# Four paddings ahead of the second score region, two moved steps and a new order of the last list in an attention kernel

## The chip, the cores and the metric

One Trainium2 chip, one of its cores. The metric is the device time of one execution in microseconds (us); lower is better. Several runs of a kernel are summarised by their median. A profile shows one further execution: the time that each instruction took on TensorE (PE for matmuls, PEld for weight loads), VectorE (DVE), ScalarE (ACT), GpSimd (POOL) and the queue of SyncE (SP), which here issues nearly all transfers.

## The reference

Attention with many query heads and one shared key and value head, between two layer norms, added to the input. All is float32.

```python
# x (64, 128, 512); Wq (512, 1024): 16 heads of 64; cond (64, 64): rows 0 and 1 are the null key
# and value, and it stands for Wkv (512, 128); attn_bias (16, 128, 128); mask (64, 128); Wo (1024, 512)
xn = layernorm(x, g_in)
q = (xn @ Wq).reshape(b, n, H, DH).transpose(0, 2, 1, 3) * DH ** -0.5
k, v = split(xn @ Wkv)
k, v = concat([null_key, k], 1), concat([null_value, v], 1)
sim = einsum('bhid,bjd->bhij', q, k) + concat([null_bias, attn_bias], -1)
sim = where(causal_mask, neg, sim)
sim = where(mask (the null column is always allowed), sim, neg)
out = einsum('bhij,bjd->bhid', softmax(sim), v)
return x + layernorm(out.reshape(b, n, H * DH) @ Wo, g_out)
```

## The kernel before

There are B = 64 batch entries of 128 tokens. The kernel works on them in pairs, in cycles `c`: while cycle `c` does the softmax of the batches 2c and 2c+1, it also projects the queries of a later group of four batches, does the output projection of the pair before, the final norm of the pair before that, and loads and normalises tokens five pairs ahead. The order of all of it is written out by hand: each engine runs its instructions in the order of the source, and an engine waits where another has not yet delivered.

- `cycle(c)` is one such pass for c = 1 to 29. It ends in `region(c)`: the scores of the batches 2c+2 and 2c+3 (`heads`, line 651) and the values of 2c and 2c+1 (`values_one`, line 770), 128 and 112 PE matmuls on 64- and 32-row tiles of the array, of which several run at a time. `region(-1)` and `region(0)` stand in a front part that is written out apart; region(0) is the second run of scores.
- Projections use Strassen's scheme: `q_one(c, k, h)` is product `k` of seven for the queries, `out_one(p, k)` product `k` of seven for the outputs of the pair `p`. In the cycles from LEAF = 2 on three of the query products are split once more (`leaf(c, k, stage)`, matmuls on line 553, additions by DVE on line 556). In the first two cycles the products 1, 6, 7 and 4 of `q_one` (line 597) are accumulated in one PSUM bank, `pa`, and ACT copies the bank between them (lines 608 and 614).
- One matmul of the source is four PE instructions, two weight loads and two matmuls; one output product has four such matmuls, `q_half` and `kv_mm` too, one query product has two, and the stages 0 to 3 of a leaf have one, three, two and one.
- The softmax of a half `hf` of a batch is `scores_max` (DVE), `exps` (ACT, line 701, eight rows), `rinv` (DVE, a reciprocal, line 718), `scale` (POOL, line 722); then `blocks_T` (DVE, line 737) transposes the batch for the values. `bias_add` (POOL, line 635) prepares the scores' bias.
- Tokens go through DVE's 32x32 transposes, one store of a group to DRAM (`tokens_out`, 1 MB, line 340) and loads back (`tokens_in`). In the front, `tokens_out(2)` is the last statement before `region(0)`.
- `nc.tensor.addr_align(256, offset=n)` pads PE's instructions with fillers (NOP in the profile) until the next one stands at place `n` of a block of 256. Three stand in the front (lines 1397, 1406, 1419), at 30, 71 and 135; one in each cycle (line 1240), at 133, 129, 143 and 152 in the cycles 1 to 4, at 141 in the last and at 159 in the others, ahead of `leaf(c, 4, 1)`.
- After the last cycle a hand-written list finishes the last eight batches. Their output norm is `pair_stats` (DVE: statistics, line 909, their aggregation, 911, and a sum, 913), `pair_pow` (POOL, 917), `pair_center` (DVE, line 942: subtract the mean, multiply by the gain `gob`), `pair_scale` (DVE, line 948: scale, add the residual `res`), `store`. The functions `gain_copy` (ACT copies the gain to a PSUM bank, which `pair_center` then reads) and `stats_part` (the statistics of half a row) exist, but are not called.

Of the kernel before, what the change touches and what calls it, by code (L numbers as in the profile page):

```python
# [17 lines left out]
def kernel(  # L18
# [940 lines left out]
    def store(b):  # L959
        nc.sync.dma_start(out=out[b], in_=ys.pop(b))  # L960
# [12 lines left out]
    def q_one(c, k, h):  # L973
        i = 2 * c + 4 + h
        g, f = divmod(i, GB)
        if g >= NG:
            return
        if k == 1 and f % FH == 0:
            q_tile(g, f // FH)
        if k == 1:  # L980
            product(g, f, 1, ps_q, "a")
            if c >= LEAF:
                first_into(g, f, 0)
            else:
                keep("a", "p1")
        elif k == 2:
            product(g, f, 2, ps_w, "w")
            q_out(g, f, lo_t, "w", "p1")
        elif k == 5:
            product(g, f, 5, ps_q, "c")  # L990
        elif k == 6:
            product(g, f, 6, ps_q, "a", start=False)
            if c >= LEAF:
                first_into(g, f, 1)
            else:
                keep("a", "u2")
        elif k == 7:
            product(g, f, 7, ps_q, "a", start=False)
            if c >= LEAF:
                first_into(g, HC + f, 0)  # L1000
                nc.vector.tensor_tensor(
                    q_part(g, HC + f, 1), by_block("c"), q_part(g, HC + f, 0), ALU.add
                )
            else:
                keep("a", "u3")
                q_out(g, HC + f, hi_t, "c", "u3")
        elif k == 8:
            o = q_part(g, f, 1)
            nc.vector.tensor_tensor(o, by_block("c"), o, ALU.add)
        elif k == 3:  # L1010
            product(g, f, 3, ps_q, "c", start=False)
            q_out(g, f, hi_t, "c", "u2")
        else:
            product(g, f, 4, ps_q, "a", start=False)
            q_out(g, HC + f, lo_t, "a")

    def out_one(p, k, dve=False):
        if not 0 <= p < B:
            return
        if k == 1:  # L1020
            out_product(p, 1, ps_y, "X")
            out_keep("yp1", 1, dve)
        elif k == 2:
            out_product(p, 2, ps_w, "w")
            out_part(p, 0, "w", "yp1")
        elif k == 6:
            out_product(p, 6, ps_y, "X", start=False)
            out_keep("yu2", 2, dve)
        elif k == 5:
            out_product(p, 5, ps_y, "Y")  # L1030
        elif k == 7:
            out_product(p, 7, ps_y, "X", start=False)
            out_keep("yu3", 1, dve)
            out_part(p + 1, 1, "Y", "yu3")
        elif k == 4 and at_end:
            out_product(p, 4, ps_w, "w")
            out_part(p + 1, 0, "w", "yu3")
        elif k == 3 and at_end:
            out_part(p, 1, "Y", "yu2")
            out_product(p, 3, ps_w, "w")  # L1040
            o = y_half(p, 1)
            nc.vector.tensor_tensor(o, prod["yw"], o, ALU.add)  # L1042
# [28 lines left out]
    def cycle(c):  # L1071
# [70 lines left out]
            mask_neg(n0 // GB)  # L1142
        if c >= LEAF:
            q_one(c, 8, 0)
        out_one(p, 2)
        if toks:
            norm_stats(m)
        if soft:
            exps(b0, 1, 0, 6)
        if c < LEAF:  # L1150
            q_one(c, 4, 0)
        q_one(c, 1, 1)
        if c >= LEAF:
            leaf(c, 2, 1)
# [67 lines left out]
            blocks_T(b0)  # L1222
        if fin:
            store(r + 1)
        if soft:
            rinv(b1, 1)
            scale(b1, 1)
        q_one(c, 5, 1)
        if c >= LEAF:
            leaf(c, 4, 0)  # L1230
        q_one(c, 7, 1)
        if c >= LEAF:
            q_one(c, 8, 1)
# [3 lines left out]
            bias_add(n0)  # L1237
        out_one(p, 7)
        if soft:
            nc.tensor.addr_align(256, offset={1: 133, 2: 129, 3: 143, 4: 152, B // 2 - 3: 141}.get(c, 159))  # L1240
        if c >= LEAF:
            leaf(c, 4, 1)
        if soft:
# [172 lines left out]
    tokens_T(9)  # L1416
    leaf_weights(2, 2)
    q_one(0, 6, 1)
    nc.tensor.addr_align(256, offset=135)
# [43 lines left out]
    scores_max(B - 4, 1)  # L1463
    exps(B - 4, 0, 0, 8)
    scores_upper(B - 2, ps_w, "ww")
    exps(B - 4, 1, 0, 8)
    scores_add(B - 2, 1)
    scores_max(B - 3, 1)
    out_one(B - 6, 1, True)
    rinv(B - 4, 0)  # L1470
    out_one(B - 6, 2)
    out_sum(B - 6, 1)
    out_sum(B - 6, 2)
    scores_add(B - 2, 0)
    scale(B - 4, 0)
    rinv(B - 4, 1)
    scores_max(B - 2, 0)
    exps(B - 3, 0, 0, 8)
    scores_upper(B - 1, ps_s, "s")
    scale(B - 4, 1)  # L1480
    out_one(B - 6, 5)
    scores_add(B - 1, 1)
    load_res(B - 6)
    exps(B - 3, 1, 0, 8)
    scores_add(B - 1, 0)
    blocks_T(B - 4)
    out_sum(B - 6, 3)
    out_one(B - 6, 6, True)
    rinv(B - 3, 0)
    scores_max(B - 2, 1)  # L1490
    scale(B - 3, 0)
    load_res(B - 5)
    rinv(B - 3, 1)
    pair_stats(B - 8)
    out_one(B - 6, 3)
    banks = value_banks(B - 4, True)
    scale(B - 3, 1)
    blocks_T(B - 3)
    values_one(B - 4, 0, banks)
    exps(B - 2, 0, 0, 8)  # L1500
    values_out(B - 4, (0, 2))
    values_out(B - 4, (1, 3))
    scores_max(B - 1, 0)
    rinv(B - 2, 0)
    out_one(B - 6, 7, True)
    out_one(B - 6, 4)
    exps(B - 2, 1, 0, 5)
    values_one(B - 3, 1, banks)
    values_out(B - 3, (0, 2))
    scale(B - 2, 0)  # L1510
    pair_pow(B - 8)
    values_out(B - 3, (1, 3), True)
    out_sum(B - 4, 0)
    exps(B - 2, 1, 5, 8)
    pair_stats(B - 7)
    rinv(B - 2, 1)
    exps(B - 1, 0, 0, 8)
    scores_max(B - 1, 1)
    banks = value_banks(B - 2, True)
    out_one(B - 4, 1, True)  # L1520
    scale(B - 2, 1)
    rinv(B - 1, 0)
    blocks_T(B - 2)
    pair_center(B - 8)
    out_one(B - 4, 2)
    pair_scale(B - 8)
    store(B - 8)
    exps(B - 1, 1, 0, 8)
    out_sum(B - 4, 1)
    out_one(B - 4, 5)  # L1530
    out_sum(B - 4, 3)
    rinv(B - 1, 1)
    pair_stats(B - 6)
    pair_stats(B - 5)
    out_one(B - 4, 6)
    out_one(B - 4, 3)
    values_one(B - 2, 0, banks)
    out_sum(B - 4, 2)
    scale(B - 1, 1)
    values_out(B - 2, (0, 2), True)  # L1540
    pair_pow(B - 7)
    scale(B - 1, 0)
    values_out(B - 2, (1, 3))
    pair_pow(B - 5)
    blocks_T(B - 1)
    pair_center(B - 7)
    out_one(B - 4, 7)
# [81 lines left out]
```

## Time and profile before

| | before |
|---|---|
| median of 3 runs | 1040.87 us (1039.3 to 1042.82) |
| the profiled execution | 1039.45 us, its span 1037.7 us |
| PE busy | 1018.7 us, 98% |
| PEld busy | 894.7 us, 86% |
| DVE busy | 862.6 us, 83% |
| POOL busy | 788.3 us, 76% |
| ACT busy | 644.2 us, 62% |
| mean granted clock of PE | 0.996 |

The span runs from the first to the last instruction; the execution's own time has 1.75 us more around it. The busy time of an engine is the time in which at least one of its instructions ran. PEclk is the clock that PE was granted, as a share of full speed. In rows of groups, "x6 | 7.1, 1191 | 0.0" reads: six instructions, 7.1 us busy in all, 1191 ns each in the mean, 0.0 us of idle time before them; in rows of a timeline, start and duration in us, engine, line, operation, output and inputs, and in brackets the idle time before it and what ended that. In the list of waits, "a <- b: 5.3, 14, 0.5" is the total in us, how many, and the longest. In a table of stretches the columns are named in its head, "(x129)" counting instructions.

### The profile page before, as it was taken

To read this page: it belongs to the slowest core of one execution; us is meant where nothing else is said; L and a number is where in the kernel's file an instruction comes from. 1 tells how busy PE (TensorE), PEld (TensorE's weight loads), DVE (VectorE), ACT (ScalarE), POOL (GpSimd) and SP (SyncE) were. 2 spreads that over 40 slices of the span, in tenths; PEclk is the share of its full clock that TensorE was granted. 3 is DMA by queue.
4 is the path that set the end of the run, shared out by engine and by line. 5 is a ranking of instruction groups with operands and counts; after the bars stand their busy time and mean duration, and the time that the engine had idled before them with its cause. 6 is when DMAs were issued, how large, how long until landed. Compare 5 with 4: busy or idle time off the path is not lost. (4 is left out here: it accounts for less than half of the span.)

```text
span 1037.7 us, 31779 instructions
## 1 busy us (share of the span) xinstructions
PE 1018.7 (98%) x12104; PEld 894.7 (86%) x12104; DVE 862.6 (83%) x1996; ACT 644.2 (62%) x2743; POOL 788.3 (76%) x710
## 2 busy tenths in 40 slices
PE   8989999999999999999999999999999999999996
PEld 7878888888888888888888888898888898888875
DVE  7765888888888888888888888888888988878788
ACT  3646765557765657756557765567755567765581
POOL 3697959779595886968779596886968779596774
PEclk9999999999999999999999999999999999999999
DMA  6551151531606225051431615225151441502202
GB/s 211 162 129 48 52 136 53 138 101 73 161 17 160 69 92 146 32 156 53 130 109 72 148 31 148 81 85 153 33 156 53 130 109 73 125 13 63 83 11 92
DMA packets 70263, 100.90 MB, mean 97 GB/s; under 512 B 27744, under 2 KB 31328, under 8 KB 68320
## 3 DMA queue, kind: packets, MB, share of 16 engines
q1 hardware_dynamic: 69008, 97.83, 33.5%
q8 instruction: 96, 1.57, 0.7%
q10 hardware_dynamic: 1104, 1.05, 0.3%
q14 instruction: 55, 0.45, 0.1%
HBM read 63.19 MB, written 33.55 MB: 93 GB/s over the span
## 5 line engine op out<-in xcount | busy, mean ns | idle before, releaser
L701 ACT ACTIVATE s<-s,nmax 128x65 f32<-128x65 f32 (+1 forms) x1024 | 377.0, 401 | 3.2 <-DVE nmax L692 3.2
L701 ACT ACTIVATION_READ_ACCUMULATOR s<-s,nmax 128x1 f32 x1024 | 229.8, 224 | 0.0
L722 POOL TENSOR_TENSOR s<-s,rinv 128x1024 f32<-128x1024 f32 (+1 forms) x128 | 188.3, 1481 | 50.5 <-DVE rinv L718 49.8
L635 POOL TENSOR_TENSOR s<-biasp,mneg 128x1552 f32<-128x1552 f32 x64 | 204.9, 3223 | 2.3 <-DMA x<-in_x_dram 2.0
L810 ACT ACTIVATE oT<-poX,nv 128x256 f32<-128x256 f32 x59 | 28.0, 475 | 224.3 <-PE poX L770 117.8
L556 DVE TENSOR_TENSOR qT<-pl,qT 128x128 f32<-128x128 f32 (+1 forms) x420 | 128.5, 329 | 9.1 <-PE pl L553 6.6
L687 DVE TENSOR_TENSOR s<-ps,s 128x256 f32<-128x256 f32 (+2 forms) x224 | 120.1, 606 | 15.9 <-PE ps L651 15.2
L860 PE MATMUL pyX<-wo,oT 128*128 128x256 f32 x512 | 121.6, 380 | 0.3 <-POOL oT L843 0.3
L692 DVE TENSOR_REDUCE nmax<-s 128x8 f32<-128x520 f32 (+1 forms) x128 | 118.9, 950 | 0.0
L860 PE MATMUL pyX<-wT,oT 128*128 128x256 f32 x488 | 115.5, 380 | 0.3 <-POOL oT L843 0.3
L737 DVE STREAM_TRANSPOSE sb<-s 128x1536 f32<-128x1536 f32 x64 | 112.9, 1765 | 0.5 <-POOL s L722 0.5
L860 PEld LDWEIGHTS pyX<-wo,oT 128*128 128x128 f32 x512 | 96.7, 190 | 15.4 <-issue 1.3
L917 POOL TENSOR_TENSOR rstdo<-rstdo,nhalf 128x1 f32<-128x1 f32 x64 | 36.7, 574 | 81.9 <-PE pl L553 70.0
L860 PEld LDWEIGHTS pyX<-wT,oT 128*128 128x128 f32 x488 | 88.4, 190 | 10.4 <-POOL oT L843 0.7
L651 PE MATMUL ps<-kT,qT 64*64 64x128 f32 (+1 forms) x4096 | 93.6, 245 | 0.7 <-issue 0.7
L651 PEld LDWEIGHTS ps<-kT,qT 64*64 64x64 f32 x4096 | 85.5, 134 | 5.7 <-issue 2.4
L289 POOL TENSOR_TENSOR rstd<-rstd,nhalf 128x1 f32<-128x1 f32 x64 | 37.3, 584 | 67.4 <-DVE rstd L288 65.4
L770 PE MATMUL pos<-sb,vr 32*64 32x128 f32 (+1 forms) x1792 | 83.8, 325 | 2.8 <-issue 2.8
L770 PE MATMUL poY<-sb,vr 32*64 32x128 f32 x720 | 76.7, 352 | 0.0
L770 PE MATMUL poX<-sb,vr 32*64 32x128 f32 x960 | 75.7, 304 | 0.0
L503 ACT COPY qT<-pa 128x256 f32<-128x256 f32 x168 | 66.7, 397 | 1.4 <-PE pa L597 1.4
L860 PE MATMUL pyw<-wo,oT 128*128 128x256 f32 x280 | 66.3, 379 | 0.6 <-POOL oT L843 0.6
(147 smaller groups left out, 2514.5 us busy)
## 6 DMA issues: line engine op xcount, KB each, us to landing
res<-in_x_dram SPq DMA_DIRECT2D x64, 256.0 KB, 3.1
out_dram<-y SPq DMA_DIRECT2D x58, 256.0 KB, 2.0
x<-in_x_dram SPq DMA_DIRECT2D x224, 64.0 KB, 2.7
xd<-xb SPq DMA_DIRECT2D x14, 1024.0 KB, 3.9
xT<-xd SPq DMA_DIRECT2D x56, 256.0 KB, 5.7
vr<-vd SPq DMA_DIRECT2D x64, 128.0 KB, 2.7
x<-in_x_dram SPq DMA_DIRECT2D x8, 256.0 KB, 4.8
vd<-vt SPq DMA_DIRECT2D x32, 64.0 KB, 2.2
```

What stands on the lines that cost most here:

```text
L289: nc.gpsimd.tensor_tensor(rstd, rstd, nhalf, ALU.pow)
L503: nc.scalar.copy(q_part(g, c, h), by_block("a"))
L556: nc.vector.tensor_tensor(o, p, o, ALU.add)
L635: nc.gpsimd.tensor_tensor(S[b], biasp, mneg[:, t].unsqueeze(1).broadcast_to([P, R8, ROW]), ALU.add,)
L651: nc.tensor.matmul(to[r][i * DH : (i + 1) * DH, f, :], qT[g, f // FH, t // GH][rows, f % FH, t % GH, NQ - 1 - i if hf else i], kT[g][rows, ...
L687: nc.vector.tensor_tensor(sv, ps, sv, ALU.add)
L692: nc.vector.tensor_reduce(nmax[b][:, hf], S[b][:, :, WITH_NULL[hf]], AX.X, ALU.max, negate=True)
L701: nc.scalar.activation(row, row, AF.Exp, bias=nmax[b][:, hf, k : k + 1], accum_out=rsum[b][:, hf, k : k + 1],)
L722: nc.gpsimd.tensor_tensor(sv, sv, rinvs.pop((b, hf)).unsqueeze(2).broadcast_to([P, R8, sv.shape[2]]), ALU.mult,)
L737: nc.vector.transpose(sb.rearrange("p j e q -> p e j q"), S[b][:, :, 1 : ROW - 1].rearrange("p e (j k) -> p e j k", k=Q),)
L770: nc.tensor.matmul(po[s][rows, half], vr[g][quad(s), j, t, :], sb[quad(s), slots, r * NF : (r + 1) * NF, :], start=start, stop=True, skip_ ...
L860: nc.tensor.matmul(prod[key], h[:, c, :], w[:, c, :], start=(start and c == 0), stop=(c == HC - 1), skip_group_check=not start,)
```

## The change

- In the front the three paddings go to 31, 73 and 138, and a fourth, to 179, is put ahead of `q_half(2, 1)`.
- In the cycles the paddings 133, 129, 143 and 152 become 159 like the others.
- In `cycle`, `q_one(c, 4, 0)`, which only the second cycle (c = 1) has, moves ahead of `out_one(p, 2)`, `norm_stats` and six exponentials. The reciprocal `rinv(b1, 1)` and its `scale` move behind `q_one(c, 5, 1)` and `leaf(c, 4, 0)`.
- The list behind the last cycle has a new order. It now calls `gain_copy()` once, behind the values of B - 1, and `stats_part` for the last two batches; `values_out(B - 6, (0, 2))` and the evacuation in `out_one(B - 4, 7)` go from ACT to DVE, those in `out_one(B - 4, 1)` from DVE to ACT; `load_res(B - 6)`, which takes one of two buffers that the residuals of B - 8 and B - 7 hold, now stands behind `load_res(B - 5)`, which takes the other; PE's only new order is `out_one(B - 4, 3)` behind `values_one(B - 2, 0)`.

```diff
@@ -1142,13 +1142,13 @@
             mask_neg(n0 // GB)
         if c >= LEAF:
             q_one(c, 8, 0)
+        else:
+            q_one(c, 4, 0)
         out_one(p, 2)
         if toks:
             norm_stats(m)
         if soft:
             exps(b0, 1, 0, 6)
-        if c < LEAF:
-            q_one(c, 4, 0)
         q_one(c, 1, 1)
         if c >= LEAF:
             leaf(c, 2, 1)
@@ -1222,12 +1222,12 @@
             blocks_T(b0)
         if fin:
             store(r + 1)
-        if soft:
-            rinv(b1, 1)
-            scale(b1, 1)
         q_one(c, 5, 1)
         if c >= LEAF:
             leaf(c, 4, 0)
+        if soft:
+            rinv(b1, 1)
+            scale(b1, 1)
         q_one(c, 7, 1)
         if c >= LEAF:
             q_one(c, 8, 1)
@@ -1237,7 +1237,7 @@
             bias_add(n0)
         out_one(p, 7)
         if soft:
-            nc.tensor.addr_align(256, offset={1: 133, 2: 129, 3: 143, 4: 152, B // 2 - 3: 141}.get(c, 159))
+            nc.tensor.addr_align(256, offset={B // 2 - 3: 141}.get(c, 159))
         if c >= LEAF:
             leaf(c, 4, 1)
         if soft:
@@ -1394,7 +1394,7 @@
     rinv(1, 0)
     q_half(0, 1)
     scale(1, 0)
-    nc.tensor.addr_align(256, offset=30)
+    nc.tensor.addr_align(256, offset=31)
     q_one(0, 4, 0)
     exps(1, 1, 0, 4)
     exps(1, 1, 4)
@@ -1403,7 +1403,7 @@
     rinv(1, 1)
     q_one(0, 3, 0)
     scale(1, 1)
-    nc.tensor.addr_align(256, offset=71)
+    nc.tensor.addr_align(256, offset=73)
     q_one(0, 1, 1)
     q_one(0, 2, 1)
     out_weight_sum(0)
@@ -1416,13 +1416,14 @@
     tokens_T(9)
     leaf_weights(2, 2)
     q_one(0, 6, 1)
-    nc.tensor.addr_align(256, offset=135)
+    nc.tensor.addr_align(256, offset=138)
     q_one(0, 5, 1)
     q_one(0, 7, 1)
     out_weight_sum(1)
     values_send(1)
     norm_apply(10)
     norm_apply(11)
+    nc.tensor.addr_align(256, offset=179)
     q_half(2, 1)
     blocks_T(1)
     bias_add(3)
@@ -1447,145 +1448,150 @@
         cycle(c)
     at_end.append({})
 
-    load_res(B - 4)
-    load_res(B - 3)
+    scores_lower((B - 2, B - 1))
+    scores_max(B - 4, 0)
+    values_out(B - 6, (1, 3))
     load_res(B - 2)
-    load_res(B - 1)
-    values_out(B - 6, (1, 3))
-    values_out(B - 6, (0, 2))
-    scores_max(B - 4, 0)
-    scores_max(B - 3, 0)
-    bias_add(B - 1)
-    scores_lower((B - 2, B - 1))
+    values_out(B - 6, (0, 2), True)
     values_out(B - 5, (1, 3), True)
     values_out(B - 5, (0, 2), True)
-    out_sum(B - 6, 0)
     scores_max(B - 4, 1)
...
     values_one(B - 1, 1, banks)
+    pair_stats(B - 4)
+    store(B - 8)
     values_out(B - 1, (0, 2))
-    pair_center(B - 5)
+    pair_pow(B - 7)
+    pair_center(B - 7)
     pair_scale(B - 7)
-    store(B - 7)
     values_out(B - 1, (1, 3))
-    pair_stats(B - 4)
-    pair_stats(B - 3)
+    gain_copy()
     pair_pow(B - 6)
     out_one(B - 2, 1)
-    out_sum(B - 2, 0)
-    out_sum(B - 2, 1)
+    store(B - 7)
+    pair_stats(B - 3)
     pair_center(B - 6)
     out_one(B - 2, 2)
+    out_sum(B - 2, 0)
+    pair_center(B - 5)
+    out_sum(B - 2, 1)
     out_sum(B - 2, 3)
     pair_pow(B - 3)
     pair_center(B - 3)
-    pair_pow(B - 4)
     pair_scale(B - 6)
     store(B - 6)
+    pair_scale(B - 3)
+    store(B - 3)
     pair_scale(B - 5)
     store(B - 5)
+    pair_pow(B - 4)
+    out_sum(B - 2, 2)
     pair_center(B - 4)
-    pair_scale(B - 3)
-    store(B - 3)
     out_one(B - 2, 5)
+    pair_scale(B - 4)
+    store(B - 4)
     out_one(B - 2, 6)
     out_one(B - 2, 3)
-    pair_scale(B - 4)
-    store(B - 4)
-    out_sum(B - 2, 2)
+    stats_part(B - 2, 0)
+    stats_part(B - 2, 1)
     pair_stats(B - 2)
     pair_pow(B - 2)
     pair_center(B - 2)
     pair_scale(B - 2)
-    store(B - 2)
     out_one(B - 2, 7)
     out_one(B - 2, 4)
+    stats_part(B - 1, 1)
+    stats_part(B - 1, 0)
     pair_stats(B - 1)
     pair_pow(B - 1)
+    store(B - 2)
     pair_center(B - 1)
     pair_scale(B - 1)
     store(B - 1)
```

More of the change, by code (lines that the diff above doesn't have):

```diff
@@ L1224, in cycle @@
             store(r + 1)
+        q_one(c, 5, 1)
+        if c >= LEAF:
+            leaf(c, 4, 0)
         if soft:
@@ L1227, in cycle @@
             scale(b1, 1)
-        q_one(c, 5, 1)
-        if c >= LEAF:
-            leaf(c, 4, 0)
         q_one(c, 7, 1)
@@ L1448 @@
     at_end.append({})
-    load_res(B - 4)
-    load_res(B - 3)
+    scores_lower((B - 2, B - 1))
+    scores_max(B - 4, 0)
+    values_out(B - 6, (1, 3))
     load_res(B - 2)
-    load_res(B - 1)
-    values_out(B - 6, (1, 3))
-    values_out(B - 6, (0, 2))
-    scores_max(B - 4, 0)
-    scores_max(B - 3, 0)
-    bias_add(B - 1)
-    scores_lower((B - 2, B - 1))
+    values_out(B - 6, (0, 2), True)
     values_out(B - 5, (1, 3), True)
     values_out(B - 5, (0, 2), True)
-    out_sum(B - 6, 0)
     scores_max(B - 4, 1)
+    scores_upper(B - 2, ps_w, "ww")
+    scores_max(B - 3, 0)
     exps(B - 4, 0, 0, 8)
-    scores_upper(B - 2, ps_w, "ww")
+    load_res(B - 4)
+    load_res(B - 1)
     exps(B - 4, 1, 0, 8)
     scores_add(B - 2, 1)
+    bias_add(B - 1)
+    load_res(B - 3)
     scores_max(B - 3, 1)
     out_one(B - 6, 1, True)
-    rinv(B - 4, 0)
-    out_one(B - 6, 2)
+    out_sum(B - 6, 0)
     out_sum(B - 6, 1)
     out_sum(B - 6, 2)
+    rinv(B - 4, 0)
+    rinv(B - 4, 1)
     scores_add(B - 2, 0)
-    scale(B - 4, 0)
-    rinv(B - 4, 1)
     scores_max(B - 2, 0)
     exps(B - 3, 0, 0, 8)
[L1479 to L1483, printed above, removed]
+    scale(B - 4, 0)
     exps(B - 3, 1, 0, 8)
     scores_add(B - 1, 0)
+    out_one(B - 6, 2)
+    scores_upper(B - 1, ps_s, "s")
+    out_one(B - 6, 5)
+    scale(B - 4, 1)
+    out_sum(B - 6, 3)
+    scores_add(B - 1, 1)
     blocks_T(B - 4)
-    out_sum(B - 6, 3)
     out_one(B - 6, 6, True)
     rinv(B - 3, 0)
+    load_res(B - 5)
+    scale(B - 3, 0)
     scores_max(B - 2, 1)
-    scale(B - 3, 0)
-    load_res(B - 5)
+    exps(B - 2, 0, 0, 8)
     rinv(B - 3, 1)
+    scale(B - 3, 1)
+    load_res(B - 6)
+    out_one(B - 6, 3)
     pair_stats(B - 8)
-    out_one(B - 6, 3)
+    pair_pow(B - 8)
     banks = value_banks(B - 4, True)
-    scale(B - 3, 1)
-    blocks_T(B - 3)
     values_one(B - 4, 0, banks)
-    exps(B - 2, 0, 0, 8)
     values_out(B - 4, (0, 2))
     values_out(B - 4, (1, 3))
-    scores_max(B - 1, 0)
-    rinv(B - 2, 0)
+    blocks_T(B - 3)
     out_one(B - 6, 7, True)
@@ L1507 @@
     exps(B - 2, 1, 0, 5)
+    exps(B - 2, 1, 5, 8)
+    rinv(B - 2, 0)
+    scale(B - 2, 0)
     values_one(B - 3, 1, banks)
+    scores_max(B - 1, 0)
     values_out(B - 3, (0, 2))
-    scale(B - 2, 0)
-    pair_pow(B - 8)
     values_out(B - 3, (1, 3), True)
     out_sum(B - 4, 0)
-    exps(B - 2, 1, 5, 8)
-    pair_stats(B - 7)
     rinv(B - 2, 1)
     exps(B - 1, 0, 0, 8)
+    out_one(B - 4, 1)
+    pair_stats(B - 7)
     scores_max(B - 1, 1)
-    banks = value_banks(B - 2, True)
-    out_one(B - 4, 1, True)
+    exps(B - 1, 1, 0, 8)
+    pair_center(B - 8)
     scale(B - 2, 1)
     rinv(B - 1, 0)
+    out_one(B - 4, 2)
     blocks_T(B - 2)
[L1524 to L1528, printed above, removed]
     out_sum(B - 4, 1)
-    out_one(B - 4, 5)
-    out_sum(B - 4, 3)
+    banks = value_banks(B - 2, True)
     rinv(B - 1, 1)
```

17 lines of the change are left out of this document (9 added, 8 removed).

## The prediction, made before the changed kernel was run

> **What bounds the kernel now.** I read the page's head first, then a table of stretches, then the rows behind the one odd stretch, and the end last.
>
> ```profile
> span 1037.7 us, 31779 instructions
> ...
> PE 1018.7 (98%) x12104; PEld 894.7 (86%) x12104; DVE 862.6 (83%) x1996; ACT 644.2 (62%) x2743; POOL 788.3 (76%) x710
> ...
> q8 instruction: 96, 1.57, 0.7%
> ```
>
> TensorE (PE) is busy 98% of the span, the next engine 83%: what shortens PE's own time shortens the kernel, and what only another engine waits for does not. The third line is the fetch of code: 96 packets, 1.57 MB in all, thus 16 KB each, for 12104 matmuls, as many weight loads and a few hundred instructions of the sequencer, so one packet is a block of about 256. A padding sets the next instruction's place in such a block, its slot; the table compares the same work at different slots. Each pass ends in a region of 128 score matmuls and 112 value matmuls, 64 or 32 rows each, so several run at once and instructions are used up fastest there.
>
> ```profile
> core 0: us, PE busy (x) PEld busy (x) DVE busy (x) ACT busy (x) POOL busy (x), PEclk, DMA share, GB/s
> 63.95:66.79 2.84, 2.84 (x129) 2.67 (x128) 2.09 (x4) 0.00 (x0) 2.84 (x2) 1.00 0.94 355
> 66.79:67.69 0.90, 0.90 (x32) 0.44 (x28) 0.24 (x2) 0.00 (x0) 0.90 (x2) 1.00 0.47 122
> 67.69:70.36 2.67, 0.00 (x0) 0.00 (x1) 2.67 (x6) 0.00 (x0) 2.67 (x2) 0.96 0.51 118
> 70.36:74.01 3.65, 3.65 (x84) 3.10 (x84) 1.60 (x2) 0.00 (x0) 3.57 (x4) 0.56 0.98 230
> 101.04:106.66 5.62, 5.62 (x241) 4.79 (x241) 4.79 (x10) 0.00 (x0) 5.62 (x4) 1.00 0.02 6
> 132.52:138.14 5.62, 5.62 (x241) 4.88 (x240) 5.56 (x13) 0.00 (x0) 1.80 (x1) 1.00 0.36 64
> 163.97:169.54 5.57, 5.57 (x242) 4.88 (x241) 4.81 (x12) 0.00 (x0) 5.57 (x4) 1.00 0.03 7
> 195.34:200.64 5.30, 5.30 (x242) 4.71 (x241) 5.24 (x12) 0.00 (x0) 1.95 (x1) 1.00 0.43 78
> 258.45:263.74 5.29, 5.29 (x241) 4.71 (x240) 5.23 (x12) 0.00 (x0) 1.93 (x1) 1.00 0.45 99
> 195.34:227.35 32.01, 31.79 (x379) 27.39 (x378) 27.24 (x66) 20.19 (x86) 18.78 (x15) 1.00 0.55 135
> 289.49:320.58 31.09, 31.09 (x379) 27.62 (x378) 26.36 (x63) 20.20 (x86) 29.31 (x31) 1.00 0.16 61
> 320.58:352.08 31.50, 31.41 (x379) 27.47 (x378) 27.24 (x66) 20.18 (x86) 18.78 (x15) 1.00 0.56 137
> ```
>
> Rows 1 to 4 are region(0), in pieces: 2.84 + 0.90 + 2.67 + 3.65 = 10.06 us; rows 5 to 9 are regions 1, 2, 3, 4 and 6: 5.62, 5.62, 5.57, 5.30, 5.29. Region(0) thus loses 4.77 us: 2.67 in which PE does nothing, and most of the rest at a granted clock of 0.56.
>
> The code says where the gap lies. One matmul call of the source is two matmuls and two weight loads, four slots. After the padding to 135 come 2 + 2 + 4 + 4 + 2 + 2 = 16 calls, 64 slots: region(0) starts at slot 199. 256 slots of scores, one semaphore instruction and the 28 weight loads of row 2 with their 28 matmuls end at 199 + 256 + 1 + 56 = 512, exactly a block's edge. PE ran out of instructions. The same count puts regions 1 to 4 at slots 181, 197, 211, 220 and all later ones but one at 227.
>
> Why only there? The block behind an edge is fetched when the sequencer passes the edge before (slot 256, in the scores).
>
> ```profile
> 63.53 0.35 SPq L340 DMA_DIRECT2D xd<-xb  x1
> ...
> q1 hardware_dynamic: 217, 1.04, 93.9%
> ...
> q8 instruction: 1, 0.02, 27.5%
> ...
> q8 instruction: 1, 0.02, 24.6%
> ...
> q8 instruction: 1, 0.02, 28.8%
> ...
> 602.14 1.10 PE L651 MATMUL ps<-kT,qT 64*64 64x128 f32 x32
> ```
>
> The first row is SyncE's timeline: a 1 MB store is issued 0.4 us before region(0). The second is the DMA table for 64.4 to 67.5: the engines are 94% busy with it. The third is that table for 67.9 to 68.1: only then does the block's fetch move, and 2.3 us later PE resumes. The fourth (257.9 to 258.2) and fifth (602.7 to 602.9) are the fetches of two regions at slot 227, whose scores began at 258.45 and, by the last row, at 602.14; no gap followed in either. My reading: in region(0) the fetch queued behind the 1 MB.
>
> The Trainium skill, "Runtime: NRT & Kernel Launch", section Instruction fetch mechanics, says that the cost of crossing a 16 KiB boundary is "mostly hidden". By that rule this change would bring next to nothing in the front; 512 being hit exactly speaks against it here.
>
> **The change part by part** (against the profiled execution's 1039.45 us; its span is 1037.7).
>
> *Region(0).* The new padding puts slot 179 before 4 + 4 + 2 + 2 calls: 179 + 48 = 227, as in the steady regions. The edge in the scores is passed 28 instructions sooner. If, as in the row at 258, the fetch moves 0.45 us before the scores, then with scores at about 64.2 it moves near 63.75, ahead of the 1 MB (from 64.4). As late as at 602.8, 0.7 after its scores' start, it would be caught again. I take the former: like region(6) at 258, and unlike region(17), region(0) has scores that need nothing of the last few products before it. 10.06 to 5.29, **-4.77**. That the slow clock goes too rests on the row behind the gap: 0.56 after a gap of 2.67, 1.00 in all other stretches.
>
> The Trainium skill, "TensorE: Matmul & The Clock Gate", section What's actually happening, has the clock halve after about 3.4 us of idleness; the trace shows it after 2.67. If the rule held and the slow clock had another cause, 84 matmuls at 5.29's pace (2.45 us for 112) would keep their 1.8 us of loss, and the whole would come out 1.8 higher.
>
> *The pads' own cost.*
>
> ```profile
> L1419 PEldq NOP  x24: 13/13/13, 55.1 to 56.8; - x24
> ...
> 56.88 1.10 PE L597 MATMUL pc<-xS,wS 128*128 128x256 f32 x4 [0.52 <-DVE xb L331]
> ...
> 58.68 3.62 PE L437 MATMUL pq<-xT,wq 128*128 128x256 f32 x16
> ```
>
> 24 fillers take 1.7 us, 0.07 each, and PE starts right behind the last. By the slots, the three old pads grow by one filler each and the new one holds 179 - 138 - 16 = 25, some 1.85 us. They begin when the eight matmuls before them are queued, and those keep PE busy from 56.88 to 58.68. Cost between 0.2 and 2.0 on the path; I take **+0.3**, as 1.8 us of work stand over 1.85 of fillers. If that cover were gone it would be the 2.0.
>
> *The per-pass pads.* In the second cycle 12 calls, 48 slots, follow its pad, in later ones 17 calls, 68. Region 1 goes from 133 + 48 = 181 to 159 + 48 = 207, between rows of 5.62 and 5.57: nothing. Regions 2 and 3 go to 227: 0.33 + 0.28 = **-0.6**. Region 4 gains 0.01.
>
> *The moved product* (second cycle only, c = 1).
>
> ```profile
> 79.30 1.03 PE L597 MATMUL pa<-xS,wq 128*128 128x256 f32 x4
> 80.16 1.89 PE L860 MATMUL pyw<-wo,oT 128*128 128x256 f32 x8
> ...
> 83.51 0.48 PE L597 MATMUL pa<-xT,wq 128*128 128x256 f32 x1 [0.59 <-ACT qT L614]
> ...
> 80.47 0.43 ACT L608 COPY ku<-pa 128x256 f32<-128x256 f32 x1
> ```
>
> Product 4's evacuation no longer queues behind six exponentials, so the 0.59 wait goes. But product 4 adds into the bank that ACT is copying until 80.90, and the product that covered this (80.16 on) now comes after it: PE would wait from 80.16 to about 81.0, 0.8. **0**, between -0.6 and +0.3. Behind the wait are queued only PE's own products; the six exponentials start later, and their reciprocal has room.
>
> *The moved reciprocal.*
>
> ```profile
> 346.06 0.16 DVE L718 RECIPROCAL rinv<-rsum 128x8 f32<-128x8 f32 x1
> 346.14 0.23 DVE L556 TENSOR_TENSOR qT<-pl,qT 128x128 f32<-128x128 f32 x1
> ...
> 346.42 0.30 PEld L553 LDWEIGHTS pl<-xS,wq 128*128 128x128 f32 x2 [0.49 <-DVE qT L556]
> ...
> PEld pl L553 <- DVE qT L556: 5.3, 14, 0.5
> ```
>
> PE waits for the addition, which stands behind the reciprocal. Swapped, it starts 0.08 us sooner; six or so of the waits are of this kind (31.50 against 31.09 in the table): **-0.4**, between 0 and -0.5. POOL's scaling starts 0.2 later, before two bias additions with nothing near them that PE waits for.
>
> *The final list.* PE's order hardly changes, and its work not at all; DVE's tail decides.
>
> ```profile
> L942 DVE SCALAR_TENSOR_TENSOR y_end<-y_end,mvo,gob 128x512 f32<-128x512 f32 x6 | 7.1, 1191 | 0.0
> L948 DVE SCALAR_TENSOR_TENSOR y_end<-y_end,rstdo,res 128x512 f32<-128x512 f32 x6 | 4.4, 744 | 0.9 <-POOL rstdo L917 0.9
> L948 DVE SCALAR_TENSOR_TENSOR y<-y,rstdo,res 128x512 f32<-128x512 f32 x2 | 2.2, 1085 | 0.0
> ...
> 1027.05 0.42 DVE L1042 TENSOR_TENSOR y_end<-pyw,y_end 128x256 f32<-128x256 f32 x1
> 1027.28 1.89 PE L860 MATMUL pyw<-wT,oT 128*128 128x256 f32 x8
> 1033.89 0.75 DVE L948 SCALAR_TENSOR_TENSOR y_end<-y_end,rstdo,res 128x512 f32<-128x512 f32 x1 [0.44 <-POOL rstdo L917]
> ```
>
> PE is done at 1029.17, the last DVE result at 1034.64: DVE runs through its list in order. The six centerings that now read the gain from PSUM took 1191 ns each, the residual steps of the same shape 744; at 744 they save 6 x 0.45 = 2.7. No row shows a centering with a PSUM gain; if it is no faster, 0. Added to DVE ahead of the last half: one evacuation (0.35, as ACT gives it up) and residual steps that now run beside POOL's sums, which took 1085 instead of 744 (three: 1.0). Halved statistics change nothing: both halves still stand behind the last addition. -2.7 + 0.35 + 1.0 = **-1.4**, between -2.7 and +0.8 (the load of the third residual row block now waits for the second residual step; its landing can hold up DVE).
>
> Sum: -4.77 + 0.3 - 0.6 + 0 - 0.4 - 1.4 = **-6.9**: 1032.6 beside 1039.45. The median of the three runs, 1040.87, lies 1.4 above that execution, so I forecast 1034.0. Nothing should give it back: the steady passes are PE-bound (31.09 busy of 31.09).
>
> **The rivals.**
>
> *The fetch is caught again* (19%). For: the margin is 0.65 us, and the row at 602.8 is late by more. Then the 4.77 stay: -2.1, **1038.8**. Against: the row at 258.
>
> *Crossings cost nothing here* (3%), the rule above: the gap has another cause, and again 1038.8. Against: slot 512.
>
> *The waits for x become the rule* (6%), the slower case.
>
> ```profile
> DVE st L284 <- DMA x<-in_x_dram: 7.5, 12, 1.3
> ```
>
> In passes like 320.58 to 352.08 DVE waits for a token load and is then late for PE, at 0.41 us a pass, and 0.92 in the pass from 195.34. Some 22 passes are free of it. All passes begin earlier against the loads' queue; if every one fell into this, 22 x 0.92 less 6.9 is +13, at half of that +3. It decides from (6.9 + 3.1) / 22 = 0.45 a pass; I give it **1045**. Against: each load is issued in its pass's own order, so it moves along.
>
> **How the numbers follow.** My forecast has 72%: 1034.0, with -9.0 to -3.2 from the ends above, 1031.9 to 1037.7. The range reaches on to the first rival: 1031.5 to 1039.0. A measurement here tells 0.3% (3.1 us) from no change; 1037.7 is that edge. Faster: 0.72 and a little of the first rival, 0.75. Same: the rest of that and the second rival, 0.17. Slower: the third and some unnamed, 0.08.
>
> **What would show it.** Region(0) near 5.3 us with PEclk 1.00 and a code packet before 64.4; regions 2 and 3 at 5.29; fewer of the 0.25 us waits of PE for DVE's L556; a wait of 0.8 us before product 4 in the second cycle; centerings near 0.74 us and the distance from PE's end to the last DVE result shorter than 5.5. A gap of over 2 us in region(0) would prove the main term wrong; centerings still near 1.2 us the tail's.

## The result, and the profile after

The changed kernel takes 1034.44 us (median of 5 runs, 1031.49 to 1035.38), the kernel before 1040.68 us beside it (5 runs, 1039.3 to 1042.82). The ratio is 0.9934, its 95% interval 0.9915 to 0.9954: 6.2 us, or 0.66%, faster. The forecast was 1034.0, a sum of -6.9.

The profiled execution took 1035.38 us, the longest of the five, its span 1033.6. The head of its page, and then the code queue:

```profile
span 1033.6 us, 31778 instructions
...
PE 1017.9 (98%) x12104; PEld 894.1 (87%) x12104; DVE 864.3 (84%) x2000; ACT 644.0 (62%) x2742; POOL 787.5 (76%) x710
...
q8 instruction: 96, 1.57, 0.7%
```

PE is busy 0.8 us less, while the span is 4.1 us shorter: what went was mostly time in which PE stood still. These two profiles differ by less than the medians do; the section on the prediction says why in part. The code packets are as many as before. The table of stretches for regions 0, 1, 2 and 3, then for one odd and one even pass (a pass is a cycle, counted from one region's start to the next; an odd one ends in a region of odd number):

```profile
core 0: us, PE busy (x) PEld busy (x) DVE busy (x) ACT busy (x) POOL busy (x), PEclk, DMA share, GB/s
64.36:69.65 5.29, 5.29 (x241) 4.71 (x240) 4.09 (x8) 0.00 (x0) 5.29 (x3) 1.00 0.78 263
96.70:102.63 5.93, 5.71 (x242) 4.91 (x241) 5.12 (x10) 0.00 (x0) 5.93 (x4) 1.00 0.03 6
128.45:133.74 5.29, 5.29 (x241) 4.71 (x241) 5.23 (x12) 0.00 (x0) 2.12 (x1) 1.00 0.39 68
159.57:165.13 5.56, 5.56 (x242) 4.83 (x241) 4.80 (x12) 0.00 (x0) 5.56 (x4) 1.00 0.03 7
628.44:661.03 32.59, 31.84 (x379) 27.39 (x379) 27.27 (x66) 20.19 (x86) 18.70 (x15) 1.00 0.54 132
661.03:692.13 31.10, 31.10 (x379) 27.63 (x379) 26.39 (x63) 20.20 (x86) 29.82 (x31) 1.00 0.17 62
```

Region(0) takes 5.29 us instead of 10.06, has no gap and runs at full clock. The DMA table for 63.6 to 63.8 holds its code packet (first row below), 0.7 us ahead of its scores; SyncE issues the 1 MB store at 63.81 (second row), behind it.

```profile
q8 instruction: 1, 0.02, 29.5%
...
63.81 0.35 SPq L340 DMA_DIRECT2D xd<-xb  x1
```

Region(2) is at 5.29 as forecast, region(3) at 5.56 is not, and region(1) is slower (5.62 to 5.93). The odd pass of the fifth row is 1.5 us longer than a pass needs. The list of waits of the whole span shows a possible cause, and the moved product's new wait:

```profile
DVE st L284 <- DMA x<-in_x_dram: 9.4, 11, 2.0
...
PEld pl L553 <- DVE qT L556: 6.4, 14, 1.0
...
PE pa L597 <- ACT ku L608: 0.6, 1, 0.6
```

VectorE waits for token loads 9.4 us in all (7.5 before), and PE for VectorE's additions 6.4 us, 14 times (5.3 before, 14 times). The end, as groups, as POOL's last power, and as VectorE's last addition and last result:

```profile
L948 DVE SCALAR_TENSOR_TENSOR y_end<-y_end,rstdo,res 128x512 f32<-128x512 f32 x6 | 5.6, 943 | 0.7 <-POOL rstdo L917 0.4
L942 DVE SCALAR_TENSOR_TENSOR y_end<-y_end,mvo,gain 128x512 f32<-128x512 f32 x6 | 4.3, 737 | 0.0
L948 DVE SCALAR_TENSOR_TENSOR y<-y,rstdo,res 128x512 f32<-128x512 f32 x2 | 2.8, 1382 | 0.1
...
1029.23 0.55 POOL L917 TENSOR_TENSOR rstdo<-rstdo,nhalf 128x1 f32<-128x1 f32 x1 [2.77 <-DVE rstdo L913]
...
1024.32 0.42 DVE L1042 TENSOR_TENSOR y_end<-pyw,y_end 128x256 f32<-128x256 f32 x1
1029.84 0.75 DVE L948 SCALAR_TENSOR_TENSOR y_end<-y_end,rstdo,res 128x512 f32<-128x512 f32 x1
```

From the last addition to the last result it is 6.27 us (1024.32 to 1030.59), before 7.59 (1027.05 to 1034.64).

### The profile page after: what moved, and what is told of

Read it like the earlier page. It is cut to its first block, busy times and chain, and to the rows that moved or that the text cites. A ratio compares the mean times of both kernels' runs of the same rounds, so it can differ in the third digit from the quotient of the medians.

```text
span 1033.6 us, 31778 instructions
## 1 busy us (share of the span) xinstructions
PE 1017.9 (98%) x12104; PEld 894.1 (87%) x12104; DVE 864.3 (84%) x2000; ACT 644.0 (62%) x2742; POOL 787.5 (76%) x710
## 5 line engine op out<-in xcount | busy, mean ns | idle before, releaser
L556 DVE TENSOR_TENSOR qT<-pl,qT 128x128 f32<-128x128 f32 (+1 forms) x420 | 128.6, 329 | 9.5 <-PE pl L553 6.9
```

Of the source, the lines that this page charges most:

```text
L556: nc.vector.tensor_tensor(o, p, o, ALU.add)
```

## The experiments

Four came first: the paddings alone, all but the paddings, the store at another place, and the list alone.

**The paddings alone.**

```diff
 (the kernel before)
-    nc.tensor.addr_align(256, offset=30)
+    nc.tensor.addr_align(256, offset=31)
...  71 to 73, 135 to 138
+    nc.tensor.addr_align(256, offset=179)
     q_half(2, 1)
...
-  offset={1: 133, 2: 129, 3: 143, 4: 152, B // 2 - 3: 141}.get(c, 159)
+  offset={B // 2 - 3: 141}.get(c, 159)
```

> The kernel before with the four front paddings and the paddings of the cycles 1 to 4 of the changed kernel, and nothing else. Theory (the paddings carry the gain, by taking region(0)'s code fetch out from behind the 1 MB store): region(0) 10.06 to about 5.3 us without a gap and without half clock, region(1) up by 0.3 (5.9, as in the changed kernel), regions 2 and 3 together down by 0.3; about -4.8 us in all, less what the waits for x give back: between -4.8 and -3. Rival (block edges cost nothing, the gain comes from the steps and the list): within 1 us of the kernel before, the gap of 2.67 us stays somewhere in the front.

Measured: 1035.24 us against 1040.33, ratio 0.9952 (0.9939 to 0.9965), -5.1 us. Regions 0 and 1:

```profile
64.73:70.02 5.29, 5.29 (x241) 4.71 (x240) 4.09 (x8) 0.00 (x0) 5.29 (x3) 1.00 0.82 263
97.03:103.12 6.09, 5.70 (x241) 4.90 (x240) 5.26 (x10) 0.00 (x0) 6.09 (x4) 1.00 0.02 5
```

The paddings carry most of the gain, and region(1) is slower by them alone. The median lies just past the expected band, on the side of more gain.

**All but the paddings.** The changed kernel with the seven old paddings and without the fourth.

> The changed kernel with the paddings of the kernel before. Theory: region(0) is back near 10 us with its gap of about 2.7 and its half clock, and only the list, the reciprocal and the moved product are left: -1 to -1.8 us against the kernel before. Rival (the list and the steps carry the gain): -4 us or more, region(0) short.

Measured: 1039.45 us against 1040.33, ratio 0.999 (0.9979 to 1.0001); region(0) 9.75 us, at a clock of 0.82 in the mean. The rest of the change is worth about 0.9 us, a little under the expected band, and the interval just reaches zero.

**The store behind region(0) in the source.**

```diff
-    tokens_out(2)
     region(0)
+    tokens_out(2)
```

> The kernel before, with the 1 MB store issued behind region(0) instead of ahead of it; all slots as before, region(0) at 199 and its second edge at exactly 512. Theory A (the fetch of the block behind 512 is asked for at 256, in the scores, and waits behind the 1 MB): with the queues empty region(0) takes 5.3 to 5.9 us, no gap over 0.6 and no half clock; about -4.5 us, if the loads that follow the store are not late. Rival B (the edge at 512 itself, where it falls between the last weight load and the last matmul of a row of scores, or the prefetch depth there): the gap of 2.67 us and 10.06 stay with free queues. Rival C (both): a gap of 1 to 2 us.

Measured: 1041.17 us, ratio 1.0005 (0.9994 to 1.0016), region(0) 9.52 us. SyncE's timeline shows that the experiment changed nothing:

```profile
63.73 0.35 SPq L340 DMA_DIRECT2D xd<-xb  x1
```

Region(0) issues no transfer, so on SyncE's queue the store has the same neighbours as before, and goes out 0.4 us ahead of the scores again. The run tells none of the theories apart.

**The list alone.** The kernel before with the new list behind the last cycle, `gain_copy()` and `stats_part` included, and nothing else.

> The kernel before with the new order of the final list, its gain copied to PSUM and the half statistics, nothing else. Theory: from the start of region(29) to the end about 1.0 us shorter, as between the two profiles: the last addition to the last result 7.59 to 6.3, the centerings 1191 to about 740 ns, GpSimd's power 0.99 to 0.55, but the list no earlier at its last addition; in all -1.0 us. As forecast: -1.4. Rival (the list's gain in that pair of profiles was chance, a new wait for the residual load eats it): 0 or above.

Measured: 1039.63 us against 1040.33, ratio 0.9991 (0.9978 to 1.0004). In its profile the last addition to the last result takes 6.26 us, the centerings 736 ns. The direction is as expected; a size of 1 us is below what the times of these runs tell apart. Their profiles do: from the end of region(29) to the end of the span the old list takes 54.49 to 54.53 us in the five profiles that have it, the new one with its gain in PSUM 53.60 to 53.71 in eight.

**The store behind the x loads.** The same question, asked so that the store does move: it now has transfers of the second cycle ahead of it.

```diff
-    tokens_out(2)
     region(0)
...  in cycle(c), behind load_x(m):
         if c == 1:
+            tokens_out(2)
             tokens_in(2)
```

> The kernel before with the 1 MB store moved on SyncE's queue behind the mask and the four x loads of the second cycle, so issued at about 67 us instead of 63.5; all slots as before, region(0) at 199, its second edge at 512. Theory A (the fetch waits behind the 1 MB): the code packet moves before 66 instead of 67.8 to 68.3, the gap of 2.7 to 3.0 us at the 28th values pair falls under 1 us, no half clock, region(0) 5.3 to 6.3; the token loads that need the store come 3 us later and may cost something in the second cycle. Rival B (the edge at exactly 512 makes the gap, whatever the queues do): the gap stays at 2.7, region(0) 9.5 to 10.4.

Measured: 1036.32 us against 1039.4, ratio 0.9973 (0.9961 to 0.9984). SyncE's timeline, then region(0) in three stretches, region(2), and the DMA table for 66.1 to 66.3:

```profile
63.20 1.71 SPq L128 DMA_DIRECT2D x<-in_x_dram  x4
65.02 0.36 SPq L340 DMA_DIRECT2D xd<-xb  x1
...
63.87:67.27 3.40, 3.40 (x157) 3.11 (x156) 2.31 (x4) 0.00 (x0) 3.40 (x2) 1.00 0.79 256
67.27:68.43 1.16, 0.34 (x9) 0.00 (x0) 0.84 (x3) 0.00 (x0) 1.16 (x2) 1.00 0.89 358
68.43:70.60 2.17, 2.17 (x84) 1.70 (x84) 2.17 (x4) 0.00 (x0) 2.17 (x3) 1.00 0.16 57
129.04:134.87 5.83, 5.83 (x241) 4.88 (x240) 5.77 (x13) 0.00 (x0) 1.72 (x1) 1.00 0.37 68
...
q8 instruction: 1, 0.02, 31.3%
```

The store moved by 1.5 us only (63.53 to 65.02), as the loads are issued fast. That was enough to see the dependence: the code packet moved at 66.2 instead of 68.0, PE resumed at 68.43 instead of 70.36, both 1.8 to 1.9 us sooner, and the 84 matmuls behind the gap took 2.17 us at full clock instead of 3.65 at 0.56. Region(0) is at 6.73. Theory A holds in its mechanism, and PE's gap is under 1 us as expected (0.83: matmuls still run for 0.34 of the 1.16 in the second row). The rest was too hopeful: the packet came at 66.2, not before 66, and region(0) is past 6.3. From 63.2 to 66.2 us the queues moved 0.49 MB, the x loads and the start of the store among it; which of them held the packet, the run doesn't tell. Rival B, the edge by itself, falls: slots and edge are unchanged.

**A token load one cycle earlier.**

```diff
 (the changed kernel, in cycle(c))
-        if m < B:
+        if m < B and (first or c == 1):
             load_x(m)
...
         if m + 1 < B:
             load_x(m + 1)
+        if first and m + 2 < B:
+            load_x(m + 2)
```

> The changed kernel, but the first token load of each odd cycle is issued in the cycle before, behind its second load, where SyncE's queue is idle, and so lands ahead of the 1 MB of loads of the odd cycle. Theory (VectorE's waits for x gave back part of the gain): the waits of VectorE's statistics for x, 0.2 to 2.0 us each in ten or eleven odd cycles, go, those cycles fall from up to 32.6 to 31.04 us, and the kernel gains 1.5 to 3.5 us over the changed one: 1031 to 1033. Rival (those waits are met by slack before the scores, or the odd cycles wait for the next load too): no change, 1034.5.

Measured: 1030.38 us (1030.22 to 1031.08) against 1039.4, ratio 0.991 (0.9894 to 0.9926): 4.1 us below the changed kernel's median. Its waits for x, and the pass that took 32.59 us above:

```profile
DVE st L284 <- DMA x<-in_x_dram: 0.8, 2, 0.4
...
PEld pl L553 <- DVE qT L1009: 0.5, 1, 0.5
...
625.62:656.66 31.04, 31.04 (x380) 27.64 (x379) 27.32 (x66) 20.31 (x86) 19.23 (x15) 1.00 0.56 140
```

Every pass from region(4) to region(28) now lies within 0.02 us of 31.04 (odd) or 31.10 (even). The gain is 0.6 us past the expected band. With VectorE's waits for x went all of PE's waits at L553 for L556's additions: the second row is the only one left of a leaf's weights. The runs lie within 0.9 us, those of the changed kernel within 3.9; in the three later kernels with this load and several runs it is 1.5 to 2.5, so these waits make a part of the scatter. Where they come from shows in SyncE's, VectorE's and PE's timelines of the changed kernel:

```profile
630.91 4.34 SPq L348 DMA_DIRECT2D xT<-xd  x4
...
636.94 7.11 SPq L128 DMA_DIRECT2D x<-in_x_dram  x8
...
644.30 0.69 DVE L284 BATCH_NORM_STATS2 st<-x 128x6 f32<-128x512 f32 x1 [1.98 <-DMA x<-in_x_dram]
...
645.98 0.49 PE L553 MATMUL pl<-xL,wq 128*128 128x128 f32 x2 [0.59 <-DVE qT L556]
```

In odd passes 1 MB of tokens comes back ahead of the x loads. In this one its four transfers landed from 636.1 to 640.3, and the first x load, issued from 636.94 on, only at 644.28, when VectorE's wait ends.

**The second cycle's region at slot 227 too.** The changed kernel with `{1: 179, B // 2 - 3: 141}.get(c, 159)`.

> The changed kernel with the padding of the second cycle at 179 instead of 159, so that region(1) starts at slot 227 and not 207. Theory (what counts is how far in the scores the first edge lies: at 207 it is 49 instructions in, behind the 32nd, whose successors wait for projections just made, so that the fetch is asked for late): region(1) 5.3 to 5.55 instead of 5.9 to 6.1, PE's longest gap in it 0 to 0.2 instead of 0.5 to 0.66; the pad 20 fillers longer, at 0.07 each up to 1.4 us, if nothing covers it. In all -0.5 to +1.0 against the changed kernel. Rival (region(1) is slow for another reason, whatever the slot): 5.9 stays.

Measured: 1033.74 us against 1039.4, ratio 0.9938 (0.9923 to 0.9954). Region(1):

```profile
96.88:102.17 5.29, 5.29 (x241) 4.71 (x240) 4.46 (x9) 0.00 (x0) 5.29 (x4) 1.00 0.01 3
```

Its code packet moves 1.5 us before the scores' start (1.1 after it at slot 207), and the stall is gone. The median is 0.7 below the changed kernel's, within the scatter of both. From region(0)'s start to region(1)'s it takes 32.34 us in both kernels, so the 20 more fillers cost nothing that shows.

**The gain from SBUF.** The changed kernel without `gain_copy()`.

> The changed kernel without the copy of the gain to PSUM, so that the six last centerings read it from SBUF as before. Theory (the PSUM gain is what shortens the tail): centerings 1190 instead of 740 ns, GpSimd's powers that run beside them 0.99 instead of 0.55, last addition to last result back from 6.3 to 7.2 to 7.6 us, the kernel 0.9 to 1.4 us slower than the changed one. Rival (the order of the list shortens the tail): centerings slower, the end no later than 0.3 us.

Measured: 1035.72 us against 1039.4, ratio 0.9961 (0.9946 to 0.9976). The same rows of the end:

```profile
L942 DVE SCALAR_TENSOR_TENSOR y_end<-y_end,mvo,gob 128x512 f32<-128x512 f32 x6 | 5.9, 989 | 0.0
...
1029.59 0.92 POOL L917 TENSOR_TENSOR rstdo<-rstdo,nhalf 128x1 f32<-128x1 f32 x1 [2.68 <-DVE rstdo L913]
...
1024.32 0.42 DVE L1042 TENSOR_TENSOR y_end<-pyw,y_end 128x256 f32<-128x256 f32 x1
1030.55 0.75 DVE L948 SCALAR_TENSOR_TENSOR y_end<-y_end,rstdo,res 128x512 f32<-128x512 f32 x1 [0.44 <-POOL rstdo L917]
```

The centerings are not at 1190 each: four took 737 to 752 ns from SBUF too, and two, with POOL at work nearly all along, 1209 and 1750. The power takes 0.92 to 0.99 us instead of 0.55, and VectorE waits 0.44 for it, twice. From the last region's start to the span's end it takes 63.81 us; 62.32 with the PSUM gain, and 63.32 in the kernel before. Without region(29) itself, which varies from 8.5 to 9.4 us, it is 55.12, 53.60 and 54.53: so the PSUM gain saves 1.5 us and the new order by itself costs 0.6. The theory holds in sign and size; the 1190 is a mix of two durations.

The last four experiments repeat parts with the early load, which takes nearly all of these waits away. Kernels that have it are called quiet from here on.

**The kernel before with the early load.** x_early's edit on the kernel before.

> The kernel before, with only the first token load of each odd cycle issued one cycle earlier, as in x_early. Theory (the waits for x are in both kernels, and hid part of the change by chance of how loads fall): its odd cycles drop from up to 32.0 to 31.04 us, in its profile 3.4 us in all, so about 1036.5 to 1037.5; against x_early (1030.4) the change is then worth 6 to 6.7 us on this quiet ground, region(0) 4.8, regions 1 to 3 0.3 to 0.6, the end 1.0. Rival (the waits for x came with the change and the kernel before has hardly any to lose): 1039.5 to 1040.5, and the changed kernel simply has a new cost.

Measured: 1036.41 us against 1039.61, ratio 0.9961 (0.9945 to 0.9976). Its waits for x (one in the front, where both of x_early's are, and one in a pass that took 31.03 us all the same), and its regions 0 and 3:

```profile
DVE st L284 <- DMA x<-in_x_dram: 1.7, 2, 0.8
...
64.29:73.98 9.69, 6.98 (x241) 5.54 (x240) 6.60 (x11) 0.00 (x0) 9.69 (x6) 0.88 0.83 234
163.91:170.15 6.24, 5.71 (x241) 4.87 (x241) 5.45 (x13) 0.00 (x0) 5.73 (x4) 1.00 0.02 5
```

The waits for x were in the kernel before as well, worth 3.2 us. With 1036.41 the gain is just past the expected band. Between the two quiet kernels the change is worth 6.0 us (1036.41 to 1030.38).

**Both: the early load and slot 227.** x_early with the second cycle's padding at 179.

> x_early with region(1) at slot 227 too (padding of the second cycle 179). Theory: region(1) 5.58 to 5.29, the longer pad covered as in second_227, all regions 0 to 28 at 5.29: -0.3 against x_early, 1030.1. Rival (the pad shows or the load queue shifts): 1030.4 or later.

Measured: 1030.14 us (1029.79 to 1032.15) against 1039.61, ratio 0.9907 (0.9892 to 0.9923). Regions 0 to 28 all take 5.29 or 5.30 us. It is the fastest kernel of the study, though not told apart from x_early by time; the place of the gain (region(1) 5.58 to 5.29) is seen in the profiles.

**The two moved steps undone.** x_early with the product and the reciprocal in their old places.

> x_early with the product of the second cycle and the reciprocal back in their old places. As forecast: the reciprocal's 0.25 us waits are back at leaf(c, 4, 1), +0.4 us, the product 0. Rival (the undisturbed cycles are 31.04 and 31.10 us long in both kernels, so the wait that shrank is made up before the region): 0, 1030.4.

Measured: 1030.21 us (1029.61 to 1031.07), against 1030.38 for x_early and 1030.14 for early_227. The list of waits has no wait of PE for L556 with either order; of PE's waits for a leaf's weights it keeps one:

```profile
PEld pl L553 <- DVE qT L1001: 0.4, 1, 0.4
```

The rival holds: the passes are as long with the old order (31.03 and 31.09), and from region(0)'s start to region(1)'s, where the product stands, it is 32.30 us (32.34 in x_early).

**Region(0) at slot 207.** x_early with the fourth front padding at 159 instead of 179.

> x_early with the fourth front padding at 159 instead of 179: region(0) starts at slot 207, its first edge 49 instructions in the scores instead of 29, its second edge inside a row of values and no longer exactly at a row's end. Theory (the fetch is asked for when the first edge is passed, and by then the 1 MB is in the queues): the code packet moves 3 us or more after the scores' start, gap over 2 us, region(0) 8 to 10. Rival A (only the exact hit of 512 was bad): 5.3 to 5.6. Rival B (as region(1) at 207 without a store: packet 1.1 after the start, gap 0.5): 5.6 to 6.1.

The only run took 1037.39 us. Region(0) in three stretches, and the DMA table for 68.4 to 68.6:

```profile
64.52:67.90 3.38, 3.38 (x153) 3.09 (x152) 2.31 (x4) 0.00 (x0) 3.38 (x2) 1.00 0.89 315
67.90:70.93 3.03, 0.13 (x8) 0.00 (x0) 2.78 (x6) 0.00 (x0) 3.03 (x3) 0.86 0.58 131
70.93:74.97 4.04, 4.04 (x88) 3.14 (x88) 1.51 (x2) 0.00 (x0) 3.90 (x4) 0.50 1.02 223
...
q8 instruction: 1, 0.02, 29.6%
```

Region(0) is at 10.45 us, past the expected 8 to 10. The packet moves 4.0 us after the scores' start, PE resumes 2.4 us later. Both rivals fall: the exact hit of a row's end at 512 does not matter, and 20 slots decide over 5 us.

## Why the prediction was right, point by point

Between the profiles of the two quiet kernels, before_x_early and x_early, the spans differ by 6.19 us (1034.86 to 1028.67), and the sum can be checked term by term:

| term | forecast | measured between the quiet profiles |
|---|---|---|
| region(0) | -4.77 | -4.75 (start of region(0) to start of region(1), 37.09 to 32.34) |
| the pads' own cost | +0.3 | +0.59 (region(-1) to region(0), 30.41 to 31.00), of it about 0.2 by the pads |
| regions 1 to 3 | -0.6 | -0.70 (region(1) to region(4), 94.57 to 93.87) |
| moved product | 0 | 0 |
| moved reciprocal | -0.4 | 0 |
| final list | -1.4 | -0.89 (end of region(29) to the end, 54.50 to 53.61) |
| in no term | | -0.44 (the front up to region(-1) -0.42; region(4) to the end of region(29) -0.02) |

So the main term was right in mechanism and size, and it carries the result. The reciprocal and the list were taken 0.9 us too high; that the sum lies within 0.7 us of the medians' -6.2 is in part luck. One step of the range doesn't add up: the upper ends given for the terms (-4.77 + 2.0 - 0.6 + 0.3 + 0 + 0.8) make -2.3, not -3.2, so the upper edge should have been 1038.6, which the stated range to 1039.0 still holds.

**Region(0).** The reading was right and is now shown: the fetch waits behind the store, and the gap follows the packet (2.35 us from packet to PE before, 2.26 with the store behind the loads, 2.40 at slot 207). In the six profiles whose packet moves 3.6 us or more after the scores' start, it takes 36.71 to 38.34 us from region(0)'s start to region(1)'s; at slot 227 it is 32.30 to 32.34. The argument by slot 512 was right in where PE runs dry, and wrong as a reason why it does: at slot 207 the edge lies elsewhere in the values and the loss is as large. What decides, as these runs read, is whether the scores pass the first edge before the store is in the queues; when the block is asked for, no row shows. The Trainium skill's rule that crossings are mostly hidden ("Runtime: NRT & Kernel Launch", Instruction fetch mechanics) holds for the regions at slot 227 and not behind a 1 MB store, where the crossing cost 4.75 us.

*The clock.* In the kernel before it fell at 70.16, 2.47 us after PE's last matmul, and stayed at 0.50 for 3.41 us. The prediction's "1.00 in all other stretches" misses the 0.96 in the row of the gap, where it fell. In all six profiles with a gap of 2.3 to 2.9 us in region(0) it fell, between 1.7 us after the gap's start and 0.8 us after its end, for 3.41 us or for 6.83; with the 0.83 us of store_behind it stayed at 1.00. The Trainium skill's rule on the clock ("TensorE: Matmul & The Clock Gate", What's actually happening), halving after about 3.4 us of idleness, does not fit the traces as it stands: none of these gaps is that long, and in the 3.41 us ahead of the fall PE had worked for 0.94 us in the kernel before and for 0.8 to 1.8 in all six.

**The pads' own cost.** The 0.59 is not all theirs: x_early's profile has a wait of VectorE for x in that stretch. Of the profiles without one, the five with the old front pads take 30.31 to 30.44 us there and the four with the new pads 30.50 to 30.53, so the pads cost about 0.2 us and were covered as forecast.

**Regions 1 to 3.** The sum was about right, the shares were not. "Region 1 ... nothing" failed: at slot 207 it took 5.93 (5.55 to 6.28 in the other five profiles), at slot 181 5.29 to 5.66; its packet moves 0.9 to 1.7 us after the scores' start at both. The new slot costs 0.4 us in the mean, and region(3), 5.57 to 6.24 with the old pad, gains 0.6 in the mean instead of 0.28: the two errors nearly cancel, by luck. Between the profiles of the two kernels themselves the three regions take 16.81 and 16.78 us, so nothing was gained there. Region(3) needed 5.56 in the changed kernel, its packet 0.8 us after the start, and 5.29 in the quiet kernels with the change, 0.2 to 0.4 us before it: slot 227 alone does not settle it.

**The moved product.** As forecast, one wait for another: the 0.59 is gone and 0.61 has come, a little less than the 0.8 expected.

**The moved reciprocal.** The step that failed is "PE waits for the addition, which stands behind the reciprocal". The reciprocal was indeed in between, but the addition was late because VectorE had waited for x earlier in that pass (0.83 us at 335.3, in the pass of the rows shown); the prediction's third rival says so of the same pass. Without that wait neither order makes PE wait, and with it PE waited 14 times in both kernels.

**The list.** The forecast took the mean of 1191 ns as each centering's price. VectorE's timeline before shows two prices:

```profile
1016.18 0.74 DVE L942 SCALAR_TENSOR_TENSOR y_end<-y_end,mvo,gob 128x512 f32<-128x512 f32 x1
...
1019.51 1.76 DVE L942 SCALAR_TENSOR_TENSOR y_end<-y_end,mvo,gob 128x512 f32<-128x512 f32 x1
```

Three took 740 to 742 ns and three 1417 to 1757, the long ones with POOL's sums of line 843 at work beside them (1.2 to 1.7 us of that time). The saving of the PSUM gain is real, 1.5 us, but half of it lies elsewhere than forecast: against gain_sbuf the last addition comes 0.77 us sooner after region(29)'s start, and the stretch behind it is 0.71 shorter, as POOL's power fell from 0.92 to 0.99 us to 0.55, which was not foreseen. Against the kernel before, from region(29)'s start to the last addition the list takes 53.05 us, 0.35 more: one residual step took 1755 ns and one 900 beside POOL, four 750 to 752 (the 943 of the table is a mean of these), and one waited 0.44 us for POOL's power. Behind the addition it is 1.3 shorter, by that power and because one scaling, that of B - 4, moved ahead of it.

**"Nothing should give it back: the steady passes are PE-bound"** was wrong of the odd passes. From region(4) to region(29) the quiet kernels need 775.6 and 775.7 us; the profile before took 779.0, that after 780.3. So in this pair of profiles the waits for x took back 1.3 us, a part of why its spans differ by 4.1 us only. Over all profiles without the early load the odd passes lose 2.6 to 5.1 us with the old front (five) and 2.2 to 5.9 with the new (four); whether the change makes them worse is not settled. The rival that they become the rule did not come true: ten passes waited for x, nine before.

## What to carry to other kernels

Where PE uses instructions fastest, look at when the code for the next block is fetched and which large transfer is issued just before: here, moving the start by 28 slots took 4.75 us from that place and moving the transfer by 1.5 us took 3.3, more than any reordering in this change. Before a wait is blamed on the instruction in front of it, follow that engine back through the pass: here a late token load, not the reciprocal, made the additions late, and issuing that load one cycle earlier gave 3.2 us on the kernel before and 4.1 on the changed one, more than all steps of the change besides the padding (0.9). A mean over six instructions may hide two prices; ask for the single ones before a saving is multiplied by six.

## What the runs showed of the hardware that was not expected

Where PE ran out of instructions, the code packet and PE's resumption lay 2.26 to 2.44 us apart in all seven profiles of region(0) with a gap, though the packet moved 2.3 us after the scores' start in one and 3.6 to 4.1 in the others. Where a region starts at slots 181 to 211, its packet moved 0.9 to 1.7 us after the scores' start without a large store, and 3.6 to 4.1 with one issued just before, in six kernels; region(0) at slot 227 had it 0.5 to 1.6 us before the start. The half clock came in stretches of 3.41 us or twice that. And a centering that reads its gain from PSUM did not slow POOL's power beside it (0.55 us, against 0.92 to 0.99 from SBUF), nor was it slowed itself (734 to 739 ns, six of six, five of them with POOL at work beside). From SBUF some were and some were not: one with POOL at work for most of its time took 752 ns, another 1750; what tells them apart, no run here shows.
